# A recurrent-gate and MoE layer on one core: VectorE's casts and scalings moved, and gate_w's second product in seven small products

## The chip, the cores and the metric

One Trainium2 chip, of which this program uses one core. A core has five engines that run their own instruction streams beside each other: TensorE (matmuls; its weight loads are listed apart), VectorE, ScalarE, GpSimd and SyncE, which here only issues DMA transfers. The profile calls them PE and PEld, DVE, ACT, POOL and SP. Matmul results land in PSUM, everything else that is computed on lies in SBUF. They wait for each other through semaphores.

The metric is the device time of one execution in microseconds (us). A profiled execution also has a span, from its first to its last instruction.

## What is computed

The input is 4 x 1024 tokens of width 1024, all in float32. The reference, cut to what matters:

```python
xn = layernorm(x)                                  # per token
# branch s: a gate, then a recurrence along the tokens
g  = sigmoid(xn @ gate_w.T + gate_b)
u_g = xn * g
s  = G * cumsum(b * u_g / G) , G = cumprod(tanh(a))
s  = c * s + (d + mean_t(u_g) @ d_lr_u @ d_lr_v / 4) * u_g
# branch g: a dense MLP, scattered by a router
gates, idx = normalized top-2 of softmax(xn @ wr.T)   # of 8 experts
h  = silu(xn @ w1.T); h = silu(h @ w3.T); h = h @ w2.T
out = zeros; out[idx[:, k]] += gates[:, k] * h      # rows 0..7 alone
y  = x + s * silu(out)
```

The scatter adds into rows 0 to 7 of the flattened tokens, so w2 is applied to a few summed rows, and all other rows of the result are a copy of x. Those eight rows lie in the first group of 1024 tokens, so the gate and the recurrence are needed for that group alone. What is left is three large float32 products: xn with w1 ("u") and the hidden layer with w3 ("m") for all four groups of 1024 tokens (sb = 0 to 3), and xn with gate_w ("g") for sb = 0.

## The kernel before

**The products.** Each product of 1024 tokens with a 1024 x 1024 matrix is done by a scheme of seven products in place of eight, with sums of blocks on both sides (numbers 1 to 7 in the code; order in line 203: for "u" and "g" 1, 2, 5, 6, 7, 4, 3, for "m" 1, 5, 6, 2, 7, 4, 3). Each of the seven is again done in seven *small products*, with sums of quarters inside ("inner sums"), or, where it is marked plain, in eight small products without inner sums. A small product is four matmuls of 128 x 128 weights with 256 columns, and each float32 matmul leaves two records in the trace, so a small product is 8 records. PLAIN_G and PLAIN_M (lines 205, 206) name the plain ones of "g" and "m".

The sums: `s1`, `s2`, `s3`, `s4` make the left-hand block sums (in SBUF, on VectorE for "u" of sb 0 and for all "m", on GpSimd for the other "u"); `left_sums` and `fresh_sums` make the inner sums of quarters (in SBUF, on GpSimd, tiles q); `first_weights` makes the right-hand block sums of w1 and gate_w for sb 0: five and seven are subtractions on GpSimd, six and four go through a copy into a spare PSUM bank by ScalarE (`with_bank`) and a subtraction on VectorE. For w1 and w3 the sums are stored to DRAM and read again for later groups; for gate_w they are used once.

**PSUM.** A small product writes a bank called X, Z or Y (two of X, two of Z, one of Y). VectorE adds each finished partial result to the running block (`first`, `more`; ScalarE copies it where nothing is to be added), and later small products of the same half accumulate in the same bank, so that they wait for that addition. The first small product of the next half with an X bank waits until the last addition out of that bank is done.

**Half** (the class that runs one of the seven) has two ways through: plain, `first` four times after two small products each; or not plain, with `first` and `more` after every small product, seven VectorE additions. In both, `whole` finishes a quarter when product 2, 4, 3, 6 or 7 completes it.

**The order.** Every instruction that goes through the wrapper of line 90 (L89 in the profile, the line of the call) keeps the order in which the program makes it, on each engine. The places are written by hand: a half has a start place, its small products come at start + 0, 2, 4, ..., and the next half starts 7 places (8 if plain) later, so that two halves run interleaved. Other work is put at places with `at(place, f)`; a generator's `yield n` moves its next step n places on. One place is half a small product. For sb 0, "g" halves start 3 places after the "u" half of the same number.

**The statistics of the next tokens.** While one group is worked on, `stats` and `squares` make mean and scale of the next group's tokens: ScalarE sums and squares whole rows, VectorE scales the sums by -1/D (lines 394 to 396), makes the variance v, and after ScalarE's root improves it in `scales` (reciprocal and three operations). TensorE transposes the 128 x 16 result st (ts), VectorE copies it out, SP stores it as flat; `norm` reads flat back as broadcast rows and VectorE normalizes the next tokens.

**The router.** `route` runs for each group: TensorE's logits plT, VectorE's max and max_index for eight columns of tokens (mx, ix), then the cast ixf of the indices, df, two sigmoids on ScalarE (g), and one-hot comparisons oh with ids. For sb 0 it stands at U[5] + 2, in the midst of product 5. The gate's sigmoid pieces (`gated`) use the same spare PSUM banks as `with_bank`.

Of the kernel before, what the change touches and what calls it, by code (L numbers as in the profile page):

```python
# [10 lines left out]
F32 = mybir.dt.float32  # L11
I32 = mybir.dt.int32
U32 = mybir.dt.uint32
AF = mybir.ActivationFunctionType
ALU = mybir.AluOpType
AX = mybir.AxisListType
P = 128
# [5 lines left out]
def kernel(  # L23
# [44 lines left out]
    NTOK, D = x.shape  # L68
    KD = D // P
    CG = wr.shape[2]  # L70
    E = 8
# [3 lines left out]
    NT = SB // P  # L75
    EPS = 1e-5
    HB = ((0, 0), (0, 1), (1, 0), (1, 1))

    class Pinned:
# [16 lines left out]
    pe, dve, act, pool, sync = (  # L96
        Pinned(e) for e in (nc.tensor, nc.vector, nc.scalar, nc.gpsimd, nc.sync)
    )

    const = ctx.enter_context(tc.tile_pool(name="const", bufs=1))  # L100
    sp = ctx.enter_context(tc.tile_pool(name="sp", bufs=1))
# [42 lines left out]
    pool.memset(ones, 1.0)  # L144
    eps = const.tile([P, 1], F32, tag="eps", name="eps")
    pool.memset(eps, EPS)

    x_first = block()
    for n in range(2):
# [34 lines left out]
    def at(place, f, *args):  # L184

        seq[0] += 1
        heapq.heappush(todo, (place, seq[0], f, args))
# [15 lines left out]
    order = {"u": (1, 2, 5, 6, 7, 4, 3), "m": (1, 5, 6, 2, 7, 4, 3)}  # L203
    line = []
    PLAIN_M = (2, 7)
    PLAIN_G = (1, 2)
    for i in order["u"]:
        line += [("u", 0, i, i == 1), ("g", 0, i, i in PLAIN_G)]
    line += [("m", 0, i, i in PLAIN_M) for i in order["m"]]
# [20 lines left out]
    def scales(o, v, sd, w):  # L230

        r0 = sp.tile([P, w], F32, tag=f"r{w}", name="r0")
        dve.reciprocal(r0, sd)
        e = sp.tile([P, w], F32, tag=f"e{w}", name="e")
        dve.scalar_tensor_tensor(e, r0, -0.5, r0, ALU.mult, ALU.mult)
        dve.tensor_mul(e, e, v)
        dve.scalar_tensor_tensor(o, e, 1.5, r0, ALU.add, ALU.mult)
# [118 lines left out]
    def stats(sb, bcs):  # L356


        sums = sp.tile([P, NT], F32, tag="sums", name=f"sums_{sb}")
        sq = sp.tile([P, NT], F32, tag="sq", name=f"sq_{sb}")  # L360
        st = sp.tile([P, 2, NT], F32, tag="st", name=f"st_{sb}")
        for n in range(NT // 2):
            xb = block()
            row = sb * SB + n * 2 * P
            sync.dma_start(
                xb.tile.rearrange("p (t h) d -> p t (h d)", t=2),
                x[row : row + 2 * P, :].rearrange("(t p) d -> p t d", p=P),
            )
            at(here[0] + 5, squares, xb, 2 * n, sums, sq, st)
            yield 9 if sb == 1 else 6  # L370
        yield 9
        v = sp.tile([P, NT], F32, tag="v8", name=f"v_{sb}")
        dve.tensor_scalar(v, sq, 1.0 / D, EPS, ALU.mult, ALU.add)
        sd = sp.tile([P, NT], F32, tag="sd8", name=f"sd_{sb}")
        act.activation(sd, v, AF.Sqrt)
        scales(st[:, 1, :], v, sd, NT)
        ts = ps_sm.tile([2 * NT, P], F32, tag="sm", name=f"ts_{sb}")
        yield 5
        pe.transpose(ts, st.rearrange("p s t -> p (s t)"), ident)
        stT = sp.tile([2 * NT, P], F32, tag="stT", name=f"stT_{sb}")  # L380
        yield 1
        dve.tensor_copy(stT, ts)
        flat = dramp.tile([2 * NT, P], F32, tag=f"flat_{sb}", name=f"flat_{sb}")
        yield 0.5
        sync.dma_start(flat, stT)
        bcs[sb] = flat

    def squares(xb, t0, sums, sq, st):
        xt = [xb[:, 2 * t : 2 * t + 2, :].rearrange("p h d -> p (h d)") for t in range(2)]
        for t in range(2):  # L390
            act.activation(xt[t], xt[t], AF.Identity, accum_out=sums[:, t0 + t : t0 + t + 1])
            yield 1
        yield 2
        dve.tensor_scalar(
            st[:, 0, t0 : t0 + 2], sums[:, t0 : t0 + 2], -1.0 / D, None, ALU.mult
        )
        yield 1
        for t in range(2):
            act.activation(
                xt[t],  # L400
                xt[t],
                AF.Square,
                bias=st[:, 0, t0 + t : t0 + t + 1],
                accum_out=sq[:, t0 + t : t0 + t + 1],
            )
            yield 1
        xb.drop()
# [32 lines left out]
    def route(sb):  # L440


        plT = ps_sm.tile([P, Q], F32, tag="sm", name=f"plT_{sb}")
        for k in range(KD):
            J, b, kt = k // 4, k // 2 % 2, k % 2
            for g in range(4):
                I, a = g // 2, g % 2
                pe.matmul(
                    plT[g * CG : (g + 1) * CG, :],
                    wr_sb[:, k, :],  # L450
                    xn[sb, I, J][:, 2 * a + b, kt * Q : (kt + 1) * Q],
                    start=(k == 0),
                    stop=(k == KD - 1),
                )
        for IJ in HB:
            xn[(sb,) + IJ].drop()
        lgT = sp.tile([P, Q], F32, tag="lgT", name=f"lgT_{sb}")
        dve.tensor_copy(lgT, plT)
        yield 2
        pl = ps_sm.tile([P, 2, P], F32, tag="sm", name=f"pl_{sb}")  # L460
        for h in range(2):
            pe.transpose(pl[:, h, :], lgT[:, h * P : (h + 1) * P], ident)
        yield 1

        N8 = 8
        lg = sp.tile([P, N8, E], F32, tag="lg", name=f"lg_{sb}")
        for h in range(2):
            dve.tensor_copy(
                lg.rearrange("p (g h) e -> p g h e", h=2)[:, :, h, :],
                pl[:, h, :].rearrange("p (g e) -> p g e", e=CG)[:, :, 0:E],  # L470
            )
        mx = sp.tile([P, N8, 8], F32, tag="mx", name=f"mx_{sb}")
        ix = sp.tile([P, N8, 8], U32, tag="ix", name=f"ix_{sb}")
        for t in range(N8):
            dve.max(mx[:, t, :], lg[:, t, :])
            dve.max_index(ix[:, t, :], mx[:, t, :], lg[:, t, :])
            if t % 2:
                yield 1
        ixf = sp.tile([P, N8, 2], F32, tag="ixf", name=f"ixf_{sb}")
        dve.tensor_copy(ixf, ix[:, :, 0:2])  # L480
        df = sp.tile([P, N8], F32, tag="df", name=f"df_{sb}")
        dve.tensor_sub(df, mx[:, :, 0], mx[:, :, 1])
        yield 1
        g = sp.tile([P, 2, N8], F32, tag="g", name=f"g_{sb}")
        act.activation(g[:, 0, :], df, AF.Sigmoid)
        act.activation(g[:, 1, :], df, AF.Sigmoid, scale=-1.0)
        oh = sp.tile([P, 2, N8, E], F32, tag="oh", name=f"oh_{sb}")
        c = cp.tile([P, N8, CG], F32, tag="C", name=f"C_{sb}")
        pool.memset(c, 0.0)
        for j in range(2):  # L490
            dve.tensor_tensor(
                oh[:, j],
                ids.unsqueeze(1).to_broadcast([P, N8, E]),
                ixf[:, :, j : j + 1].to_broadcast([P, N8, E]),
                ALU.is_equal,
            )
            yield 1
            dve.tensor_mul(
                oh[:, j], oh[:, j], g[:, j, :].unsqueeze(2).to_broadcast([P, N8, E])
            )  # L500
            yield 1
        dve.tensor_add(c[:, :, 0:E], oh[:, 0], oh[:, 1])
        gates[sb] = c
# [668 lines left out]
    for kind, sb, i, plain in line:  # L1172
        h = Half(kind, sb, i, plain)
        halves.append(h)
        S = start[kind, sb, i]
        n = 2 if sb == 0 and kind == "u" and i not in PLAIN_G else 1
        if kind != "g" and not plain:
# [6 lines left out]
    for sb in range(NS):  # L1184
        n = 2 if sb == 0 else 1
        U = {i: start["u", sb, i] for i in range(1, 8)}
        at(U[5] - (12 if sb > 1 else 7), s1, "u", sb, n)
        at(U[5] - (9 if sb > 1 else 6), s2, "u", sb, n)
        at(U[7] - 10, s3, "u", sb, n)
        at(U[3] - (12 if sb == 0 else 8.6), s4, "u", sb, n)  # L1190
        if sb == 0:
            at(U[5] + 2, route, sb)
        M = {i: start["m", sb, i] for i in range(1, 8)}
        at(M[5] - 8, s1, "m", sb, 1)
        at(M[5] - 4, s2, "m", sb, 1)
        at(M[7] - 12, s3, "m", sb, 1)
        at(M[3] - 12, s4, "m", sb, 1)
        if sb > 0:
            for r in range(6 if sb < NS - 1 else 4):
                at(U[1] + 14 * r, copy_rows, 6 * (sb - 1) + r)  # L1200
        if sb + 1 < NS:
            bcs = {}
            at(M[1] - (46 if sb == 0 else 40), stats, sb + 1, bcs)
            for k, (I, J) in enumerate(HB):
                at(M[1] + (12 if sb == 0 else 4) + 3 * k, load_xn, sb + 1, I, J, USES[I, J])
            at(M[1] + (20 if sb == 0 else 8), norm, sb + 1, bcs)
            for IJ in HB:
                at(
                    M[1] + 26,
                    lambda sb=sb, IJ=IJ: left.__setitem__(  # L1210
                        ("u", sb + 1, IJ), xn[(sb + 1,) + IJ]
                    ),
                )
# [218 lines left out]
```

## Time and profile before

| | |
|---|---|
| median of the runs | 838.4 us (838.0 to 840.01, three runs) |
| profiled execution | 839.15 us |
| its span | 837.4 us |
| mean granted TensorE clock | 0.995 |
| DMA | 194.97 MB, mean 233 GB/s |
| VectorE, SBUF additions of 128x512 (b<-b,b) | 160, 157.4 us in all, 1.00 us each |
| GpSimd, inner sums q<-b | 144, 196.3 us in all, 1.376 us each |

How to read it: the page's first part gives each engine's busy time, its share of the span and its instructions. A line of the timeline is start (us from the span's start), length (us), engine, source line, operation, output<-inputs (buffer numbers left out: b is a block, q a quarter, X_u a PSUM bank X of "u"), sizes and count; in brackets stands how long the engine had been idle and what ended it. A row of the waits is: who waited, for whom, total us, how often, longest. A row of windows has the stretch, its length, busy time and count of PE, PEld, DVE, ACT and POOL, then the granted TensorE clock (1.00 is full), the DMA share and GB/s.

### The profile page before, as it was taken

To read this page: it belongs to the slowest core of one execution; us is meant where nothing else is said; L and a number is where in the kernel's file an instruction comes from. 1 tells how busy PE (TensorE), PEld (TensorE's weight loads), DVE (VectorE), ACT (ScalarE), POOL (GpSimd) and SP (SyncE) were. 2 spreads that over 40 slices of the span, in tenths; PEclk is the share of its full clock that TensorE was granted. 3 is DMA by queue.
4 is the path that set the end of the run, shared out by engine and by line. 5 is a ranking of instruction groups with operands and counts; after the bars stand their busy time and mean duration, and the time that the engine had idled before them with its cause. 6 is when DMAs were issued, how large, how long until landed. Compare 5 with 4: busy or idle time off the path is not lost.

```text
span 837.4 us, 11277 instructions
## 1 busy us (share of the span) xinstructions
PE 823.4 (98%) x4119; PEld 704.2 (84%) x4119; DVE 549.7 (66%) x894; ACT 236.8 (28%) x386; POOL 484.8 (58%) x377
## 2 busy tenths in 40 slices
PE   8999799999999999999999999999999999999997
PEld 7888688888888878888888878888888788888885
DVE  5976879888579626665897234774994245666643
ACT  1115115656121306442112226431122030220111
POOL 0379759593898577666355753743458464574400
PEclk9999899999999999999999999999999999999999
DMA  9946335922897779928966757639875546535700
GB/s 341 421 151 225 115 126 179 361 88 89 322 401 269 264 246 340 385 95 324 408 219 225 273 192 282 239 127 405 309 248 168 201 176 239 201 139 198 306 13 2
DMA packets 56215, 194.97 MB, mean 233 GB/s; under 512 B 6512, under 2 KB 9824, under 8 KB 44256
## 3 DMA queue, kind: packets, MB, share of 16 engines
q1 hardware_dynamic: 55840, 193.71, 62.6%
q8 instruction: 33, 0.54, 0.3%
q10 hardware_dynamic: 320, 0.54, 0.2%
q14 instruction: 22, 0.18, 0.1%
HBM read 171.10 MB, written 39.87 MB: 252 GB/s over the span
## 4 chain that ended last, share of the span: by engine, by line
PE 95%; DVE 2%; DMA 2%; issue 0%; ACT 0%; SPq 0%
PE X_m L89 23%; PE X_u L89 23%; PE Z_m L89 12%; PE Z_u L89 12%; PE Y_u L89 6%; PE X_g L89 5%; PE Y_m L89 5%; PE Z_g L89 4%; PE acc L89 2%; PE plT L89 2%; DMA b<-in_x 2%; DVE ixf L89 1%; PE Y_g L89 1%; PE pp L89 0%; DVE bn L89 0%; DVE b L89 0%
## 5 line engine op out<-in xcount | busy, mean ns | idle before, releaser
L89 POOL TENSOR_TENSOR q<-b 128x512 f32<-128x512 f32 x144 | 196.3, 1376 | 232.5 <-DVE b L89 63.2
L89 ACT ACTIVATE b<-b 128x512 f32<-128x512 f32 (+1 forms) x152 | 105.0, 696 | 314.3 <-DVE b L89 310.7
L89 DVE TENSOR_TENSOR b<-b,b 128x512 f32<-128x512 f32 x160 | 157.4, 1000 | 2.9
L89 POOL TENSOR_TENSOR q<-b,q 128x512 f32<-128x512 f32 x91 | 128.3, 1413 | 10.7 <-issue 8.5
L89 POOL TENSOR_TENSOR b<-b,b 128x512 f32<-128x512 f32 x72 | 94.9, 1345 | 35.2 <-PE X_u L89 26.4
L89 PE MATMUL X_u<-q,q 128*128 128x256 f32 x432 | 102.7, 380 | 0.0
L89 DVE TENSOR_TENSOR b<-X_u,b 128x512 f32<-128x512 f32 x87 | 59.8, 689 | 63.2 <-PE X_u L89 62.5
L89 DVE TENSOR_TENSOR b<-X_m,b 128x512 f32<-128x512 f32 x84 | 57.5, 687 | 63.5 <-PE X_m L89 63.3
L89 PE MATMUL X_m<-q,q 128*128 128x256 f32 x416 | 98.4, 379 | 0.0
L89 PEld LDWEIGHTS X_u<-q,q 128*128 128x128 f32 x432 | 81.5, 190 | 14.5 <-POOL q L89 1.7
L89 POOL TENSOR_TENSOR q<-q,b 128x512 f32<-128x512 f32 x53 | 71.0, 1339 | 34.0 <-PE X_u L89 28.9
L89 PEld LDWEIGHTS X_m<-q,q 128*128 128x128 f32 x416 | 78.9, 190 | 11.6 <-issue 0.8
L89 DVE TENSOR_TENSOR b<-b,bc 128x1024 f32<-128x1024 f32 x56 | 67.7, 1211 | 5.5 <-ACT bc L89 5.4
L89 PE MATMUL X_u<-b,b 128*128 128x256 f32 x248 | 60.7, 389 | 6.1 <-ACT b L89 5.9
L89 PE MATMUL X_m<-b,b 128*128 128x256 f32 x272 | 63.5, 379 | 0.0
L89 PEld LDWEIGHTS X_u<-b,b 128*128 128x128 f32 x248 | 48.0, 194 | 13.7 <-ACT b L89 6.3
L89 PEld LDWEIGHTS X_m<-b,b 128*128 128x128 f32 x272 | 51.4, 190 | 7.4 <-ACT b L89 0.3
L89 PE MATMUL Y_u<-b,b 128*128 128x256 f32 x216 | 51.0, 379 | 0.0
L89 PE MATMUL X_u<-b,q 128*128 128x256 f32 x216 | 51.0, 379 | 0.0
L89 PE MATMUL Z_u<-q,q 128*128 128x256 f32 x216 | 51.0, 379 | 0.0
L89 PE MATMUL Z_u<-q,b 128*128 128x256 f32 x216 | 51.0, 379 | 0.0
L89 DVE TENSOR_TENSOR b<-Z_m,b 128x512 f32<-128x512 f32 x48 | 32.8, 685 | 27.2 <-PE Z_m L89 26.9
(163 smaller groups left out, 1163.9 us busy)
## 6 DMA issues: line engine op xcount, KB each, us to landing
q<-w SPq DMA_DIRECT2D x168, 256.0 KB, 3.5
b<-in_w SPq DMA_DIRECT2D x37, 1024.0 KB, 9.0
b<-w_T SPq DMA_DIRECT2D x25, 1024.0 KB, 6.5
b<-in_xT SPq DMA_DIRECT2D x15, 1024.0 KB
w<-q SPq DMA_DIRECT2D x56, 256.0 KB, 9.4
b<-in_x SPq DMA_DIRECT2D x12, 1024.0 KB
w_T<-b SPq DMA_DIRECT2D x8, 1024.0 KB, 4.3
b<-in_gw SPq DMA_DIRECT2D x6, 1024.0 KB, 13.8
```

The lines of the kernel that those rows point to most:

```text
L89: r = f(*args, **kwargs)
```

## The change

- `PLAIN_G` is now `(1,)`: product 2 of "g" is done with inner sums, in seven small products. `Half` takes the other way for it, `fresh_sums` makes its four right-hand quarters, and the left-hand quarters of "u" 2 are kept for two users (n = 2). Places after it move up by one.
- `route` no longer casts ix to ixf; the comparisons read ix itself.
- `squares` scales the sums on ScalarE, right after the second row sum; a `yield 2` goes.
- `stats` makes v on ScalarE, forms e as r0*r0*v by two VectorE products, f = 1.5 - 0.5*e on ScalarE with a constant three_halves, and st = f*r0 on VectorE; the steps are three places further apart in all. `scales` stays for sb 0.
- `s4` stands at U[3] - 13 in place of - 12 for sb 0, and at M[3] - 16 in place of - 12 for every "m".

As the built program has it: TensorE's stream loses one small product, and ts comes after two small products more; GpSimd's gets one constant and four inner sums of gate_w (one ahead of the left-hand sums of "u" 2, two in them, and one among the subtractions of product 5); on SP the store of the block of product 5 comes ahead of one store of a quarter, and flat after one load and one or two quarters. The number of table loads on ScalarE is the same.

```diff
+    three_halves = const.tile([P, 1], F32, tag="three_halves", name="three_halves")
+    pool.memset(three_halves, 1.5)
...
-    PLAIN_G = (1, 2)
+    PLAIN_G = (1,)
...
-        dve.tensor_scalar(v, sq, 1.0 / D, EPS, ALU.mult, ALU.add)
+        act.activation(v, sq, AF.Identity, scale=1.0 / D, bias=eps)
         sd = sp.tile([P, NT], F32, tag="sd8", name=f"sd_{sb}")
         act.activation(sd, v, AF.Sqrt)
-        scales(st[:, 1, :], v, sd, NT)
+        yield 1
+        r0 = sp.tile([P, NT], F32, tag="r8", name="r0")
+        dve.reciprocal(r0, sd)
+        e = sp.tile([P, NT], F32, tag="e8", name="e")
+        dve.tensor_mul(e, r0, r0)
+        dve.tensor_mul(e, e, v)
+        yield 1
+        f = sp.tile([P, NT], F32, tag="f8", name="f")
+        act.activation(f, e, AF.Identity, scale=-0.5, bias=three_halves)
+        yield 1
+        dve.tensor_mul(st[:, 1, :], f, r0)
...
-        yield 2
-        dve.tensor_scalar(
-            st[:, 0, t0 : t0 + 2], sums[:, t0 : t0 + 2], -1.0 / D, None, ALU.mult
+        act.activation(
+            st[:, 0, t0 : t0 + 2], sums[:, t0 : t0 + 2], AF.Identity, scale=-1.0 / D
         )
...
-        ixf = sp.tile([P, N8, 2], F32, tag="ixf", name=f"ixf_{sb}")
-        dve.tensor_copy(ixf, ix[:, :, 0:2])
...
-                ixf[:, :, j : j + 1].to_broadcast([P, N8, E]),
+                ix[:, :, j : j + 1].to_broadcast([P, N8, E]),
...
-        at(U[3] - (12 if sb == 0 else 8.6), s4, "u", sb, n)
+        at(U[3] - (13 if sb == 0 else 8.6), s4, "u", sb, n)
...
-        at(M[3] - 12, s4, "m", sb, 1)
+        at(M[3] - 16, s4, "m", sb, 1)
```

## The prediction

> **What bounds the kernel now.** I read the page first, then who waits for whom on TensorE, then the stretch of the one long wait, engine by engine.
>
> ```profile
> span 837.4 us, 11277 instructions
> PE 823.4 (98%) x4119; PEld 704.2 (84%) x4119; DVE 549.7 (66%) x894; ACT 236.8 (28%) x386; POOL 484.8 (58%) x377
> PE X_u L89 <- ACT b L89: 5.9, 1, 5.9
> 93.23 1.89 PE L89 MATMUL Z_g<-q,b 128*128 128x256 f32 x8
> 101.06 3.78 PE L89 MATMUL X_u<-b,b 128*128 128x256 f32 x8 [5.94 <-ACT b L89]
> 104.63 2.25 PE L89 MATMUL X_g<-b,q 128*128 128x256 f32 x8
> 106.72 0.59 PE L89 MATMUL Z_u<-q,q 128*128 128x256 f32 x2
> ```
>
> TensorE is busy for 98%, and past the first 20 us it waits for another engine for long just once: 5.9 us, at 101 us, for a ScalarE copy of X_u. Small products (8 records each) otherwise start 1.73 us apart (91.50, 93.23). So a product removed is worth 1.73 us, the wait is worth its length, and work on other engines costs nothing until it makes TensorE wait.
>
> ```profile
> 86.52 0.69 DVE L89 TENSOR_TENSOR b<-X_u,b 128x512 f32<-128x512 f32 x1 [0.80 <-PE X_u L89]
> 87.13 11.72 DVE L89 CAST ixf<-ix 128x16 f32<-128x16 uint32 x1
> 98.77 0.16 DVE L89 TENSOR_TENSOR df<-mx 128x8 f32<-128x8 f32 x1
> 98.96 0.31 ACT L89 ACTIVATE g<-df 128x8 f32<-128x8 f32 x2 [12.99 <-DVE df L89]
> 100.43 0.58 ACT L89 COPY b<-X_u 128x512 f32<-128x512 f32 x1
> 95.00:98.00 3.00, 0.12 (x1) 0.00 (x0) 3.00 (x1) 0.00 (x0) 3.00 (x4) 1.00 0.93 311
> 101.00:105.00 4.00, 3.94 (x9) 3.19 (x10) 1.82 (x7) 0.01 (x1) 0.00 (x0) 0.50 0.01 2
> ```
>
> The ScalarE copy is queued behind the gate sigmoid (g<-df), that behind df on VectorE, and df behind one cast of 16 columns that takes 11.72 us. GpSimd runs without a gap through that time and stops at 98.8; the cast ends at 98.85. The last row's clock column (0.50) shows the second half of the price: after the wait TensorE runs at half clock. X_u starts at 101.06 and not at 94.96 (93.23 + 1.73): 6.10 us. X_u and X_g then take 3.57 and 2.09 (101.06, 104.63, 106.72) where two products take 3.45: 2.21 more. The cast costs **8.31 us**.
>
> Here a rule is weighed. The Trainium skill (SBUF — State Buffer, "Who interferes with whom") counts casts among the operations that take the port pair shared with GpSimd, and says that whichever starts first keeps the pair for one whole instruction and the other blocks. By that rule the cast waits for one GpSimd addition (1.3 us), and the 11.7 us would need another cause, which the change might leave standing. The row shows it waiting past nine ends of GpSimd additions, until that engine had nothing left. I take the row: the cause is the cast. The other three casts sum to 0.5 us (12.2 in four).
>
> **Part 1, the casts go; the comparison reads ix itself.** df then follows X_u's addition by at most one GpSimd addition. The two-input comparisons cost 0.21 us each, 0.70 at most, as before. The sigmoid is done long before X_u's last product ends, so ScalarE copies X_u at once. Next late is nothing: of the inputs of the following products none is younger than 27 us when read at 101-125; with 8 us taken out, 19 are left. Gain 8.31.
>
> **Part 2, gate_w's second product as seven small ones.** One small product of TensorE goes: -1.73. Added: four GpSimd sums (1.24 apart), three VectorE additions from PSUM (0.69 each); and X_g is no longer alone between X_u's last use and the next X_u. Before, two small products of X_g and Z_g (63.32, 65.04) lie between X_u's last use in product 2 (61.59) and its first in product 5 (66.77); now gate_w's half ends in step with w1's, and one is left (1.73 us), in which VectorE must have emptied X_u.
>
> Do VectorE and GpSimd keep up there? Before, GpSimd was idle for 4.47 us, and that gap held half of VectorE's first left sums (s1):
>
> ```profile
> 45.47 8.64 POOL L89 TENSOR_TENSOR b<-b,b 128x512 f32<-128x512 f32 x7
> 58.58 1.77 POOL L89 TENSOR_TENSOR q<-b 128x512 f32<-128x512 f32 x1 [4.47 <-DVE b L89]
> 60.31 1.72 POOL L89 TENSOR_TENSOR q<-b 128x512 f32<-128x512 f32 x1
> 53.77 0.90 DVE L89 TENSOR_TENSOR b<-b,b 128x512 f32<-128x512 f32 x1
> 59.15 1.76 DVE L89 TENSOR_TENSOR b<-b,b 128x512 f32<-128x512 f32 x1
> 60.83 0.68 DVE L89 TENSOR_TENSOR b<-Z_g,b 128x512 f32<-128x512 f32 x1
> ```
>
> The ends say it. A VectorE addition with both inputs in SBUF (b<-b,b) ends 0.55 us after the GpSimd addition it met: 54.12 and 54.67, 60.35 and 60.91. GpSimd's next ends 1.12 after that (62.03). One with an input in PSUM always takes 0.68. The same section of the skill has this rule for two SBUF inputs, and it **speaks against this change**: the four new sums fill the gap.
>
> The first of the four needs a block of gate_w, which the trace has landed at 31.4, and fits in at 31.6 to 32.9, while GpSimd waits for VectorE. The other three come behind that wait (36.72 before; about 37.1 now, as VectorE's 128x128 scalings meet the first sum for 0.4 us). GpSimd's additions of the stretch then end at 54.45, 56.1, 57.8 and 59.5. Through the program's order, with 0.55 and 1.13:
> - s1's four additions end at 55.0, 56.7, 58.4, 60.0 (before 54.67, 55.27, 57.90, 58.50), with X_g's new addition between.
> - s2's first two end at 60.8 and 62.4. Only then, by the program's order, comes the addition out of X_u for the small product of 54.68, ready since 56.6: it ends at 63.0. TensorE wants X_u back at 61.59 and starts at 63.1: **new wait 1.5**.
> - s2's last two end at 64.1 and 65.8; four PSUM additions (Y_g, Z_u, X_g, X_u) follow at 0.6: 68.2. TensorE wants X_u's bank at 66.55: **new wait 1.7**.
>
> Without the rule (all at 0.69, or in a gap) both waits are nothing and the part is worth -1.73; with it, -1.73 + 3.2 = **+1.5**. The bounds: 0 below, and above 5 us, if GpSimd's next sum gets in ahead of s2 (now VectorE is first by 0.04 us, 58.54 against 58.58) and both waits grow by one addition of 1.1-1.7. I take 3.2, as both end times are rows of this trace.
>
> Do these waits cool the clock? The skill (TensorE: Matmul & The Clock Gate, Part 1) has it fall after about 3.4 us of idleness. The long wait shows 1.00 until 98 and 0.50 from 99, so some 3.5 us after the last product; the 0.66 us wait at 19.6 us shows 1.00. Waits of 1.5 and 1.7 fall on the warm side; if each were charged like the long one the sum would be 4.4 higher.
>
> On SP, the store of product 5's block now stands ahead of one 256 KB store and of the constants (wr_sb issued at 50.08) and waits for GpSimd: they slide by about 3 us, and wr_sb is read at 68.6. GpSimd's later sums come 1.5 us later. They lie 12 us or more ahead of their products from 74 us on (q at 62.03 for 74.01), so this is hidden; that cover is gone only beyond 10 us. After 98.82 GpSimd idled for 14.7 us.
>
> **Part 3, the statistics of the next tokens move.** Twelve scalings of sums (0.55 us mean, up to 1.28) and three of v (0.22) leave VectorE for ScalarE, at 0.2 us each by its 128x8 rows (g<-df). ScalarE is busy for 28%; its copies of X_u wait in places behind two 1.13 us squares more, but the last (339.27, needed at 340.80) keeps its place ahead of them. VectorE's e and st are two-input additions now: at most one GpSimd addition each, by df's rows (0.16 to 1.25). The transpose ts stands two small products later (3.45 us); st comes about 4 us later at most (202.15 to 206.2), and is wanted at 208.7. SP stores flat past one load and one or two transfers, some 4 us later; the first normalization that reads it comes 20 us after (377.7 against 398). TensorE pays 0. Cover lacking, a late st would stop TensorE for the whole delay.
>
> **Part 4, s4 sooner.** Same additions, 4 places (about 3.5 us) earlier in "m", 1 in "u". No wait of TensorE ended on them (X_m's sums are ready 13 us ahead), so no gain. The loss would be a PSUM addition behind them: in the first "m" all four now stand before X_m_7's, which moves from 252.5 to about 256.0, ends 256.7, and is wanted at 258.78. Later ones meet a thin GpSimd. 0; bounds 0 and 1. three_halves: 0.03 us of GpSimd at the start, behind what TensorE waits for.
>
> **The sum.** -8.31 - 1.73 + 3.2 = **-6.8 us**. The profiled execution took 839.15 (span 837.4 and 1.75 around it): 832.3. It lies 0.75 above the median of 838.4, so I predict **831.6**.
>
> **Rivals.**
> - The gap isn't really needed: X_u's additions escape and both new waits are 0. For: TensorE had none before; against: the two end times above. 838.4 - 10.0 = 828.4. Chance 0.10.
> - The waits grow: one GpSimd sum more in front, or the clock cools once. 831.6 + 1.8 to 4 = 833.4 to 835.6. Chance 0.07.
> - Slower: the small two-input operations of the statistics starve like the cast. GpSimd runs gapless from 204.0, so e (202.4) would wait until GpSimd itself lacks VectorE's sums (about 212.7); TensorE stops at 208.7 for ts and then for X_m behind the held s2 additions, 7.2 us with two cold clocks (2.2 each) less some overlap, 9.4: 838.4 - 6.8 + 9.4 = 841.0. It decides from 6.8 on. Against: df and e never waited for more than one addition. Chance 0.05.
> - The gain goes elsewhere: ScalarE holds X_u for another reason, or a new wait eats it. 837 to 839.5. Chance 0.05.
>
> The forecast, 830.0 to 833.2, has 0.73. The range 828.4 to 834.6 takes in most of the first two rivals. A measurement here tells 0.3% (2.5 us) from no change: faster 0.90, same 0.05, slower 0.05.
>
> **What would show it.** No cast in the page; no TensorE wait near 95 us and clock 1.00 throughout; two waits of TensorE on VectorE between 61 and 69 us, of 1.5 and 1.7; 4111 TensorE records; GpSimd's gap at 54-58 us gone. Wrong it is if these waits are missing or above 2.5 each, or if TensorE waits behind ts or in an "m" stage.

## The result and the profile after

The changed kernel took **839.58 us** (median of 20 runs, 838.42 to 840.48), the kernel before 838.28 us (20 runs, 836.90 to 840.02): ratio 1.0018, 95% interval 1.0012 to 1.0023. It is 1.3 us slower, and it lies 8 us above the 831.6 us that were predicted. Less than 0.3% is what the prediction called no change.

First the head of the page of the changed kernel, and from its view of who waits for whom the rows of TensorE's waits (total us, times, longest us):

```profile
span 838.1 us, 11267 instructions
...
PE 821.9 (98%) x4111; PEld 704.1 (84%) x4111; DVE 550.0 (66%) x878; ACT 239.8 (29%) x404; POOL 488.8 (58%) x382
```

```profile
PE X_u L89 <- ACT b L89: 5.1, 1, 5.1
PE X_u L89 <- DVE b L89: 3.6, 2, 2.2
...
PE X_g L89 <- DVE b L89: 0.5, 1, 0.5
```

The eight records of one small product are gone (4119 to 4111), and the cast is in no row. But the long wait for ScalarE's copy of X_u stands where it stood, 5.1 us in place of 5.9, and three waits for VectorE have joined it. The timeline of the changed kernel around the long wait, VectorE, then GpSimd, ScalarE and TensorE (start us, us, engine, line, operation, operands, what it waited for), and last the stretch behind the wait from its view by windows, with the clock (0.50) before the last two numbers:

```profile
88.37 0.69 DVE L89 TENSOR_TENSOR b<-X_u,b 128x512 f32<-128x512 f32 x1 [0.78 <-PE X_u L89]
88.98 11.68 DVE L89 TENSOR_TENSOR df<-mx 128x8 f32<-128x8 f32 x1
...
88.32 1.30 POOL L89 TENSOR_TENSOR q<-b,q 128x512 f32<-128x512 f32 x1
89.54 4.98 POOL L89 TENSOR_TENSOR b<-b,b 128x512 f32<-128x512 f32 x4
...
98.11 2.52 POOL L89 TENSOR_TENSOR b<-b,b 128x512 f32<-128x512 f32 x2
114.33 1.60 POOL L89 TENSOR_TENSOR q<-b 128x512 f32<-128x512 f32 x1 [13.70 <-issue]
...
100.69 0.31 ACT L89 ACTIVATE g<-df 128x8 f32<-128x8 f32 x2 [12.87 <-DVE df L89]
...
101.42 0.58 ACT L89 COPY b<-X_u 128x512 f32<-128x512 f32 x1
...
95.08 1.89 PE L89 MATMUL Z_g<-q,b 128*128 128x256 f32 x8
102.05 3.78 PE L89 MATMUL X_u<-b,b 128*128 128x256 f32 x8 [5.09 <-ACT b L89]
105.63 2.06 PE L89 MATMUL X_g<-b,q 128*128 128x256 f32 x8
...
101.00:105.00 4.00, 2.95 (x7) 2.41 (x8) 3.42 (x11) 0.70 (x2) 0.00 (x0) 0.50 0.01 2
```

**df has taken the cast's place.** A subtraction of 128x8 elements, which took 0.16 us before, now takes 11.68 us: it starts at 88.98 and ends at 100.66, when GpSimd's last subtraction ends (98.11 + 2.52 = 100.63). The chain behind it is the old one: df, sigmoid, ScalarE's copy, TensorE. X_u comes 5.24 us late (102.05 against 95.08 + 1.73) and X_g and X_u run 2.03 us longer than two products at full clock (107.53 - 102.05 against 3.45).

The same has happened a second time, in the stretch that gate_w's second product was put into (VectorE, GpSimd, TensorE):

```profile
52.44 6.08 DVE L89 TENSOR_TENSOR b<-b,b 128x512 f32<-128x512 f32 x2
...
62.64 0.68 DVE L89 TENSOR_TENSOR b<-X_u,b 128x512 f32<-128x512 f32 x1
...
53.61 3.76 POOL L89 TENSOR_TENSOR b<-b,b 128x512 f32<-128x512 f32 x3
60.40 1.77 POOL L89 TENSOR_TENSOR q<-b 128x512 f32<-128x512 f32 x1 [3.03 <-DVE b L89]
...
59.17 1.99 PE L89 MATMUL X_g<-q,q 128*128 128x256 f32 x8 [0.47 <-DVE b L89]
63.37 1.99 PE L89 MATMUL X_u<-b,q 128*128 128x256 f32 x8 [2.20 <-DVE b L89]
...
68.52 1.99 PE L89 MATMUL X_u<-b,b 128*128 128x256 f32 x8 [1.43 <-DVE b L89]
```

s1's first two additions take 6.08 us together: the first gets in only when GpSimd's run has ended (53.61 + 3.76 = 57.37) and ends 0.55 us later. The addition that frees X_u's bank comes only at 62.64. From the start of the product before these waits (56.81) to that of the one behind them (70.35) TensorE takes 13.5 us for five products, which at 1.73 us each are 8.65: the waits cost 4.9 us.

So the books of the two profiled executions are: the product -1.7, these waits +4.9, the long wait and its half clock 7.27 in place of 8.31 (-1.0), and -1.3 in the first 20 us. That makes +0.9; the last product starts 0.75 us later (832.66 against 831.91). Of the -1.3 us, 1.0 are shorter waits ahead of the acc banks (0.40 and 0.66 us before, 0.30 now), and 0.3 is a quicker start of X_u. These acc waits were between nothing and 1.1 us in the profiles of all kernels below, though the code there hardly differs.

### The profile page after: what moved, and what is told of

It reads as the page before. It is cut to its first block, busy times and chain, and to the rows that moved or that the text cites. A ratio compares the mean times of both kernels' runs of the same rounds, so it can differ in the third digit from the quotient of the medians.

```text
span 838.1 us, 11267 instructions
## 1 busy us (share of the span) xinstructions
PE 821.9 (98%) x4111; PEld 704.1 (84%) x4111; DVE 550.0 (66%) x878; ACT 239.8 (29%) x404; POOL 488.8 (58%) x382
## 4 chain that ended last, share of the span: by engine, by line
PE 94%; DVE 4%; DMA 1%; issue 0%; ACT 0%; SPq 0%
PE X_m L89 23%; PE X_u L89 22%; PE Z_m L89 12%; PE Z_u L89 11%; PE Y_u L89 6%; PE Y_m L89 5%; PE X_g L89 5%; PE Z_g L89 3%; DVE b L89 2%; PE acc L89 2%; PE plT L89 2%; DMA b<-in_x 1%; DVE df L89 1%; PE Y_g L89 1%; PE pp L89 0%; DVE bn L89 0%
## 5 line engine op out<-in xcount | busy, mean ns | idle before, releaser
L89 POOL TENSOR_TENSOR q<-b,q 128x512 f32<-128x512 f32 x93 | 130.0, 1401 | 15.9 <-issue 11.0
```

Source lines behind the costliest of these rows:

```text
L89: r = f(*args, **kwargs)
```

## The experiments

**Is it the cast, or the place?** Four kernels. Two put df, and what follows it in the first token group, seven places later (some 6 us of TensorE's work; df then starts at 99.18 in place of 88.98), so that it comes just before GpSimd's run ends: one in the changed kernel, one in the kernel before with its cast.

```diff
+        if sb == 0:
+            yield 7
         df = sp.tile([P, N8], F32, tag="df", name=f"df_{sb}")
```

> The changed kernel with the subtraction df of the first token group, and what follows from it (g, oh, C), put seven places (about 6 us) later, behind the eviction of X_u_6 and so behind GpSimd's unbroken stretch that ended at 100.63 us. Theory PLACE (whatever two-input operation inside SBUF VectorE starts in that stretch starves until it ends): df takes under 1.5 us, TensorE's wait of 5.1 us before X_u at 102.05 us and most of the half clock behind it (2.0 us) are gone, 839.6 - 7.1 = 832.5 us, between 831 and 834. Rival NEXT (something else holds the same bank as long): df is short and the time stays within 1.5 us of 839.6. Rival KIND (df starves by its own form, wherever it stands): df is again over 8 us long and the time stays at 838 to 841.

> The kernel before, its cast kept, with the cast ixf, df and what follows them in the first token group put the same seven places later. Theory PLACE: the cast takes under 1.5 us there, TensorE's wait of 6.10 us and its half clock of 2.21 us are gone, 838.3 - 8.3 = 830.0 us, between 828.5 and 832. Rival KIND (a cast between two SBUF tiles starves beside GpSimd anywhere, which is what the prediction said): the cast is again many microseconds long and the time stays at 836 or more.

The third takes the cast, and nothing else, out of the kernel before:

```diff
-        ixf = sp.tile([P, N8, 2], F32, tag="ixf", name=f"ixf_{sb}")
-        dve.tensor_copy(ixf, ix[:, :, 0:2])
...
-                ixf[:, :, j : j + 1].to_broadcast([P, N8, E]),
+                ix[:, :, j : j + 1].to_broadcast([P, N8, E]),
```

> The kernel before with the cast alone taken out, the comparisons reading ix itself; nothing else of the change. Theory PLACE: df, which is next, starves in the cast's stead from about 88 to 100 us, TensorE waits 5 to 6 us as before, 838.3 us give or take 1. Rival KIND, which is part 1 of the prediction: df follows after one GpSimd addition, 838.3 - 8.3 = 830.0 us.

The fourth sets `PLAIN_G = (1, 2)` in the changed kernel again.

> The changed kernel with gate_w's second half product given back its eight plain small products; the rest of the change stays. If the seven products cost more in new waits than they save (TensorE's waits of 2.2, 1.4 and 0.5 us between 59 and 69 us against 1.73 us of records and some 0.7 us of waits before the acc banks): 839.6 + 1.7 + 0.7 - 4.6 = 837.4 us, between 836.3 and 838.5. Rival, the prediction's terms (1.73 saved against 3.2 lost): 838.1 us. Rival GAIN (the seven products pay, the waits would have come anyway): 841.3 us.

Measured, with the kernel before at 838.57 us beside them:

| kernel | us | ratio to before, 95% |
| --- | --- | --- |
| changed, df later | 833.68 | 0.9934 (0.9920 to 0.9947) |
| before, cast and df later | 830.76 | 0.9908 (0.9895 to 0.9922) |
| before, no cast | 837.79 | 0.9990 (0.9984 to 0.9997) |
| changed, g2 plain | 837.90 | 0.9990 (0.9983 to 0.9997) |

From one set of runs to the next the kernel before took between 838.2 and 839.2 us, so a difference between kernels of different sets is good to about 1 us.

From VectorE's timelines of the kernel before without its cast, and of the kernel before with its cast later:

```profile
85.49 11.74 DVE L89 TENSOR_TENSOR df<-mx 128x8 f32<-128x8 f32 x1
```

```profile
95.86 1.38 DVE L89 CAST ixf<-ix 128x16 f32<-128x16 uint32 x1
97.16 0.16 DVE L89 TENSOR_TENSOR df<-mx 128x8 f32<-128x8 f32 x1
```

Taking the cast out of the kernel before is worth 0.8 us, not 8.3: df waits 11.74 us instead. Leaving the cast in and moving it by seven places is worth 7.8 us. The moved cast still waits for the end of GpSimd's run, but that is now only 1.35 us away. It is the place. The kernel before, with nothing changed but a delay of the cast and what follows it, is thus some 9 us faster than the changed one.

The changed kernel with df later stays above 830.8 us by 2.9. Plain products for g2 took some 2 us off the changed kernel (1.7 by the two medians, 2.0 with each set against the kernel before beside it); do the two add up? And are s1's starved additions what the seven products pay? The next two kernels both have the later df; the second also moves gate_w's four subtractions for product 5 from GpSimd to VectorE, by the way that product 6 has:

```diff
-            yield from sub(pool, b[5], b[5], b[1])
+            if kind == "g":
+                yield from with_bank(b[5], b[5], b[1])
+            else:
+                yield from sub(pool, b[5], b[5], b[1])
```

> The changed kernel with df seven places later and gate_w's second half product back at eight plain products. Theory PLACE, the two effects adding: 837.9 - 7.1 (what the later df took off TensorE's wait and half clock) = 830.8 us, between 829.8 and 831.8, the same within 0.6 as the kernel before with its cast put later (830.8). Rival COPIES (VectorE's copies and scalings that the change took out were worth something that the stall hid): clearly below that, 829 us or less. Rival G2 (the seven products pay once the stall is gone): above 833 us.

> The changed kernel with df seven places later, and with gate_w's four subtractions for its fifth product (GpSimd's at 51 to 57 us) taken by VectorE with one operand copied into a free bank by ScalarE, as the sixth product's are. Theory STARVED SUM: the first of VectorE's additions for u's fifth product starved from 52.4 to 57.9 us beside those subtractions, and this is what made TensorE wait 2.2 us before X_u at 63 us; it now starts by 54.5 us, that wait falls below 0.5 us, and the time is 833.7 - 1.9 to -2.8 = 830.9 to 831.8 us. Rival LOAD (VectorE has too much work there, whoever is beside it): the four evictions of 0.68 us that it takes over, 2.7 us, make up for it, and the time stays at 833 to 835 us.

They took **830.61** (ratio 0.9895, 0.9878 to 0.9912) and **829.20 us** (0.9877, 0.9860 to 0.9893; before 839.24 beside them). The second is 1.7 us below the range that I expected. In VectorE's and GpSimd's timelines of the second, s1 finds GpSimd at rest:

```profile
53.53 1.28 DVE L89 TENSOR_TENSOR b<-b,b 128x512 f32<-128x512 f32 x2
...
56.69 3.46 POOL L89 TENSOR_TENSOR q<-b 128x512 f32<-128x512 f32 x2 [3.35 <-DVE b L89]
```

The two additions take 1.28 us in place of 6.08, TensorE waits for no X_u or X_g in that stretch, and the seven products pay: 829.2 against 830.6, 1.4 of the 1.73 us of a product. With the stall gone and s1 starving, they had cost 3.1 us (833.68 against 830.61). 830.61 against 830.76 also says what the rest of the change is worth: these two kernels differ in the cast, the statistics and s4, and their medians in 0.15 us. They are of different sets (ratios 0.9895 and 0.9908, with intervals that overlap), so the rest is worth nothing within about 1 us.

**Can one free df where it stands?** Once by moving GpSimd's work, once by the operands. The first of the next kernels puts GpSimd's subtractions for product 7 later:

```diff
-        at(S(7) - 12, seven)
+        at(S(7) - 7, seven)
```

> The changed kernel with df where the change has it, and GpSimd's eight subtractions for the seventh products, seven of which stand in the stretch from 89.5 to 100.6 us, put five places later instead, six of them behind an instruction that waits for VectorE's sums of about 114 us. Theory PLACE (df waits for the end of GpSimd's unbroken run, so a shorter run frees it): df is done by about 93 us, after at most 4 us, TensorE's wait of 5.1 us before X_u is gone and the time is 839.6 - 7.1 = 832.5 us, with up to 3 us given back where the subtractions come to stand beside VectorE's additions of the seventh products, so 832 to 836 us. Rival OTHER RUN (GpSimd simply runs on with other work): df is again over 8 us and the time stays at 838 to 841.

Measured: **832.83 us** (0.9918, 0.9900 to 0.9935). GpSimd's run ends at 93.09, and df at 93.13, as VectorE's and GpSimd's timelines of this kernel show:

```profile
88.78 4.35 DVE L89 TENSOR_TENSOR df<-mx 128x8 f32<-128x8 f32 x1
...
90.60 2.49 POOL L89 TENSOR_TENSOR b<-b,b 128x512 f32<-128x512 f32 x2
106.86 1.59 POOL L89 TENSOR_TENSOR q<-b 128x512 f32<-128x512 f32 x1 [13.77 <-issue]
```

The second leaves GpSimd's instructions in their places, moves df by half a place, and lets ScalarE put one operand of each into PSUM (a tile fed); the comparisons, products and C follow in the same way:

```diff
+            act.copy(second, mx[:, :, 1])
+            act.copy(of, ids)
...
-        dve.tensor_sub(df, mx[:, :, 0], mx[:, :, 1])
+        dve.tensor_sub(df, mx[:, :, 0], second)
```

> The changed kernel with df, the comparisons, the products with the gates and the sum C of the first token group at their own place, but each with one of its two operands in PSUM (ScalarE copies the second maxima and the expert numbers there and writes the gates there; one product goes there too), so that none reads two SBUF tiles. Nothing is moved out of GpSimd's unbroken stretch. Theory TWO SBUF OPERANDS (an operation that reads one tile from PSUM and one from SBUF does not compete with GpSimd, as the evictions beside it show): df takes under 0.3 us at about 89 us with GpSimd running on, TensorE's wait of 5.1 us before X_u goes, 839.6 - 7.1 = 832.5 us, between 831.5 and 834. Rival SMALL OR STRIDED (the short rows of 8 elements starve whatever they read): df or a comparison is again over 8 us long and the time stays at 838 to 841.

Measured: **832.66 us** (0.9932, 0.9919 to 0.9946). In its timelines df takes 0.16 us in the middle of GpSimd's run:

```profile
90.73 0.16 DVE L89 TENSOR_TENSOR df<-mx,fed 128x8 f32<-128x8 f32 x1
...
89.58 4.97 POOL L89 TENSOR_TENSOR b<-b,b 128x512 f32<-128x512 f32 x4
```

Each of these cures with the cure for s1 makes a version that should beat both kernels:

> The changed kernel with df at its own place, GpSimd's eight subtractions for the seventh products five places later, and gate_w's fifth-product subtractions on VectorE through a PSUM bank. Both waits of TensorE in the first group should be gone, and the wait of 1.0 us before u's seventh product, which the kernels with a later df have, should not come: 829.2 - 1.0 = 828.2 us, between 827.5 and 829.2. Rival: the wait before the seventh product, or another of its size, comes again, 829.2 to 830.5 us.

> The changed kernel with the route's small operations fed from PSUM at their own place, and gate_w's fifth-product subtractions on VectorE through a PSUM bank. If both starved operations were the whole loss: 839.6 - 7.1 - 4.0 = 828.5 us, between 827.5 and 829.5, the same within 0.7 as the kernel with GpSimd's subtractions later. Rival: ScalarE's copies into PSUM or the shared banks hold something up, 830 us or more.

They took **828.28** (0.9882, 0.9867 to 0.9897) and **827.74 us** (0.9875, 0.9860 to 0.9890; before 838.17). All that TensorE still waits for in the second is this:

```profile
PE idle L89 <- POOL eps L89: 1.6, 1, 1.6
PE pp L89 <- DVE accT L89: 0.3, 1, 0.3
```

**Why does VectorE wait for a whole run there?** In each of the traces of the kernel before and the changed one, about a hundred operations with two inputs in SBUF met GpSimd and got in at its next end, or the one after. I first took it that GpSimd keeps VectorE out when its next instructions have been handed to it ahead. Both kernels put a memset of 128x8 behind each subtraction for product 7, into cells of its own, or always into the same ones:

```diff
-            yield from sub(pool, b[7], b[6], b[7])
+            for h in range(4):
+                pool.tensor_tensor(b[7][:, h], b[6][:, h], b[7][:, h], ALU.subtract)
+                pool.memset(scrap[:, 4 * (kind == "g") + h], 0.0)
+                yield 0.5
```

> The changed kernel with a GpSimd memset of 128x8 behind each of its eight subtractions for the seventh products, each into cells of its own, so that none waits for anything. df stays where the change has it, at about 89 us, and the first memset behind it comes at about 91 us. Theory RUN-AHEAD (GpSimd keeps VectorE out as long as its next instructions are already handed to it): df starves to the end of the run as before, over 10 us, and the time stays at 838.5 to 841. Rival BREAK (any GpSimd instruction that does not read two SBUF tiles lets VectorE in): df ends by 92 us, under 3.5 us, TensorE's wait of 5.1 us goes and the time is 832 to 833.5 us.

> The same with all eight memsets into the same cells, so that each has to wait until the one before it has ended[...]. Theory RUN-AHEAD: VectorE gets in at the first memset that waits, df ends by about 92 us, under 3.5 us, TensorE's wait of 5.1 us goes and the time is 832 to 833.5 us. Rival BREAK expects the same here, so the two runs together tell it apart. Rival NEITHER (what holds VectorE out is the length of the run alone, breaks or not): df is over 10 us in both and the time stays at 838.5 to 841.

They took 839.77 us (1.0009, 0.9993 to 1.0026) and 840.07 us (1.0013, 0.9995 to 1.0031), and df 11.99 and 11.98 us. My theory did not come true in the second, nor rival BREAK in either; the rival that only the run's length counts was left. The second tests my theory only weakly, though: each memset there begins some 0.05 us before the subtraction ahead of it ends, as in the first, so the chain held none of them up. (One execution of each took 832.5 and 832.9 us; there is no trace of these.) Two kernels were to give GpSimd a pause just before df, by a memset that waits for VectorE:

```diff
+        if sb == 0:
+            yield 1
+            pool.memset(lg[:, 0, 0:1], 0.0)
```

> The changed kernel with one GpSimd memset of 128x1 that waits for VectorE's last maximum, so that GpSimd pauses from about 86 to 87.6 us, some 1.7 us, and then runs its ten additions and subtractions without a gap to about 102 us. df stays at about 89 us, and so comes in the second instruction behind the pause. Theory DISTANCE (VectorE gets in when GpSimd's last pause lies few instructions back): df ends by 91.5 us, under 2.5 us, TensorE's wait before X_u at 102 us goes, 832 to 833.5 us. Rival STRETCH (these instructions keep VectorE out whatever lies before them): df takes 12 to 14 us, to about 102 us, and the time is 839.5 to 842.

> The same pause, and df four places later, behind the eviction of X_g at about 94 us, in the fifth to seventh instruction behind the pause. Theory DISTANCE with its bound between eleven and thirteen: df gets in at the next end, under 2.5 us, and the time is 832 to 834 us. Rival DISTANCE with a bound below five, or STRETCH: df lasts until GpSimd's run ends at about 102 us, 7 to 9 us; TensorE wants X_u's bank at about 97 us, and ScalarE's copy of it, in its program's order behind the gate sigmoid, waits for df, so TensorE waits about 6 us there and the time is 838 to 842.

The first took 840.25 us (1.0019, 1.0012 to 1.0026), df 11.73. It told nothing: the memset waited only for the first token's maximum, which was over, so GpSimd made no pause. In the second there was none either. df took 6.59 us to the end of the run, as the rival had it, and yet TensorE did not wait for it at all, and the time was 832.68 us (0.9930, 0.9911 to 0.9948), as the theory had it. VectorE, ScalarE and TensorE in that kernel:

```profile
94.52 6.59 DVE L89 TENSOR_TENSOR df<-mx 128x8 f32<-128x8 f32 x1
...
95.64 0.58 ACT L89 COPY b<-X_u 128x512 f32<-128x512 f32 x1 [5.36 <-PE X_u L89]
101.14 0.31 ACT L89 ACTIVATE g<-df 128x8 f32<-128x8 f32 x2 [4.92 <-DVE df L89]
...
97.16 1.89 PE L89 MATMUL X_u<-b,b 128*128 128x256 f32 x8
```

With df four places later the copy of X_u stands ahead of the gate's sigmoid in ScalarE's order, and no longer behind it. Four places thus take the whole wait away though df still starves: what cost the time was the queue behind df, and not df's length alone. In the kernels with df seven places later the copy also stands ahead of the sigmoid, so that there the rows of the cast and of df speak of the starving, and the gain in time does not by itself. The first was mended by `lg[:, N8 - 1, 0:1]`, the last token:

> As the run with the pause before df, with the memset on the last token's logits, so that it waits until VectorE's last maximum at 87.6 us: GpSimd pauses from about 86.1 to 87.6 us and then runs its ten additions and subtractions without a gap to about 102 us. df at about 89 us comes in the second or third instruction behind the pause. Theory DISTANCE: df ends by 91.5 us, under 2.5 us, and the time is 832 to 834 us. Rival STRETCH: df takes 12 to 13.5 us, to about 102 us, and the time is 839.5 to 842.

It took **832.61 us** (0.9931, 0.9911 to 0.9951). Its timelines, VectorE and then GpSimd:

```profile
88.95 1.25 DVE L89 TENSOR_TENSOR df<-mx 128x8 f32<-128x8 f32 x1
...
87.62 0.10 POOL L89 MEMSET lg<- 128x1 f32 x1 [1.71 <-DVE ix L89]
87.68 1.28 POOL L89 TENSOR_TENSOR b<-b,b 128x512 f32<-128x512 f32 x1
88.91 1.27 POOL L89 TENSOR_TENSOR q<-b 128x512 f32<-128x512 f32 x1
90.13 1.28 POOL L89 TENSOR_TENSOR q<-b,q 128x512 f32<-128x512 f32 x1
91.36 5.00 POOL L89 TENSOR_TENSOR b<-b,b 128x512 f32<-128x512 f32 x4
```

The ten GpSimd instructions that kept df out in the changed kernel (here from 90.13 on) run as free of gaps as there, but with a pause of 1.71 us two instructions ahead of them df gets in after 1.25 us, and the five comparisons, products and sums that follow it, among those ten, take 0.21 to 1.31 us.

## Why the prediction was wrong

- **Part 1 failed, in its sentence "df then follows X_u's addition by at most one GpSimd addition".** df waited for the end of GpSimd's run instead and took 11.68 us. Of the 8.31 us, taking out the cast alone brought 0.8.
- The failing step lies before that, where rule and row were weighed. The Trainium skill (SBUF — State Buffer, "Who interferes with whom") has the loser block for one whole instruction; the row showed it waiting past nine ends. From this I took "the cause is the cast". The row showed that an operation starved there, not that the kind of operation did it, and the prediction had the counter-evidence beside it: the other three casts took 0.5 us together. The same kind elsewhere doesn't starve. The rule's own words would have helped: they name two-input operations along with casts, so df was the next candidate. df's short rows (0.16 to 1.25 us) were measured after the cast had sat the run out, or beside short runs.
- "Next late is nothing" held for TensorE's inputs where df did not starve at its own place (no X_u wait after 70 us in the two last versions). The kernels with a later df have a wait of about 1 us before u's product 7, where df's followers stand among VectorE's additions.
- **Part 2: right in mechanism, too small in size.** Sum predicted +1.5; measured +3.1 once the stall is gone, and 1.7 to 2.0 beside it. Beside it, the stall itself came out 1.6 us shorter than in the changed kernel with plain g2 (7.27 against 8.91 us, by the starts of the products): one VectorE addition fewer stood between df and ScalarE's copy (0.8 us), and less was lost at half clock (0.9 us). The terms: waits of 1.5 and 1.7 were foreseen at X_u's reuse in products 2 and 5 and came as 2.20 and 1.43, with a third of 0.47 before X_g. s1's first addition was to end at 55.0 us, after one GpSimd addition; it starved to 57.9. It is the mistake of Part 1 again.
- Parts 3 and 4: predicted 0; measured nothing, within about 1 us.
- The rival "slower" had the mechanism, small two-input operations that starve like the cast, but placed it at the statistics' e, and was dismissed since "df and e never waited for more than one addition". The outcome, 839.58, lies just above what "the gain goes elsewhere" had (837 to 839.5, chance 0.05). With Part 1's gain and Part 2's true price the sum would have been 838.3 - 8.3 + 3.1 = 833.1 us, within the range.
- Of the signs named: no cast, 4111 records and the two waits (2.20 and 1.43, under the bound of 2.5) came; "no TensorE wait near 95 us and clock 1.00 throughout" failed. GpSimd's gap was not gone either, but moved and shortened (57.37 to 60.40, 3.03 us).

## What to carry to other kernels

When one instruction is many times longer than its kind, first look for the same kind elsewhere in the trace: if it is short there, what is slow is the place, and whatever is next in the queue inherits the wait. VectorE's operations with two inputs in SBUF are planned outside long unbroken runs of GpSimd, or get one operand through PSUM, or GpSimd gets a pause just ahead of them. Where none of this can be had, what TensorE waits for is put ahead of the starving chain in its engine's order. Filling an idle gap of GpSimd is not free when VectorE's additions were living in it.

## What the runs showed of the hardware

- **How long VectorE is kept out depends on how long GpSimd has run without a pause.** I counted GpSimd's instructions from its last pause, or from the last one that VectorE's getting in had stretched to 1.7 us, in all traces of this study. VectorE's two-input operations that came by the twelfth got in within two ends. Those that came from the thirteenth on (s1 at 52.4, the cast, df) waited for the run's end, over up to ten instructions. A memset between the instructions didn't count as a pause in the traces (one execution of 12 and one of 11 were 7 us faster than the rest, and no trace says why); 1.71 us without work did. Twelve instructions of 1.23 us are some 15 us, so whether instructions or time count stays open, and so does why (whether GpSimd had its instructions handed to it ahead no trace shows): only this one pause was tried.
- Operations with one operand in PSUM don't take part: 0.16 us for df in the middle of such a run.
- A wait of 2.2 us was sometimes short enough for the clock and sometimes not. In nine of the traces TensorE waits 2.20 us before the same X_u, at about 63 us. In three of them (the changed kernel, and the two with df four places later and with the real pause) the clock stayed at 1.00. In the other six it fell to a half for some 3 us, beginning between at once and 1.3 us after the product had begun (estimated from the clocks of the windows). What decides it, these runs don't show. It cost nothing here: in the changed kernel with df later the product behind it all starts at 70.19 us, in the changed kernel at 70.35, since the slowed TensorE had no second wait. Stretches of the kernel with df later, where that X_u begins at 63.22 (us, TensorE and its weight loads, VectorE, ScalarE, GpSimd, then clock, DMA share, GB/s):

```profile
63.00:64.00 1.00, 0.78 (x4) 0.70 (x5) 1.00 (x2) 0.63 (x1) 1.00 (x2) 1.00 0.00 0
64.00:65.00 1.00, 1.00 (x5) 0.86 (x4) 1.00 (x2) 0.00 (x0) 1.00 (x1) 0.76 0.00 0
65.00:66.00 1.00, 1.00 (x4) 0.72 (x4) 1.00 (x2) 0.00 (x0) 1.00 (x2) 0.50 0.00 0
```
